# Layer 1's value windows, asked for by pairs of key chunks

## The chip, the cores and the metric

The kernel runs on one core of a Trainium2 chip, in one launch, in float32. The metric is the device time of that launch in microseconds (us). Five engines work side by side: TensorE (PE in the profile, with its weight loads as PEld), VectorE (DVE), ScalarE (ACT), GpSimd (POOL) and SyncE (SP). SP issues all of this kernel's DMAs.

## The reference

Sixteen images of 64 x 64 positions with 256 channels go through two layers. Each adds an attention to its input, and each normalises the input first in groups of 8 channels.

```python
# layer 0: linear attention over all 4096 positions, 8 heads of 32
q, k, v = split(gn(x) @ w_qkv)
q = softmax(q, over the head's 32) * SCALE
k = softmax(k, over the positions)
x = x + (v^T k applied to q) @ w_out
# layer 1: every position attends to the 7 x 7 window around it, 8 heads of 32
q, k, v = gn(x) @ Wq + bq, gn(x) @ Wk + bk, gn(x) @ Wv + bv
scores = q . (unfold(k, 7) + positional embedding)
x = x + softmax(scores, over 49) applied to unfold(v, 7)
```

## The kernel before

**The image's way.** One image at a time is held in SBUF as two tiles of 128 channels x 4096 positions (`img`). Positions are ordered by columns of eight; a strip is 512 of them, 256 KB for one half of the channels. For an image the stages are: `layer0`, which takes sixteen pairs of 128 tokens (`queries_keys`, then `context`) and then adds its output; statistics and positional products; `values`, which computes layer 1's values and stores them in DRAM in `vpad`, padded; `keys_queries` and `local_attention` for the first four heads (hg 0); the same two for the last four (hg 1). The work of the next image that can be done early is put between the steps of `local_attention`.

**`local_attention`.** The image's width is cut in four units of 16 columns, taken in the order `UNITS`. A unit has nine key chunks c of eight rows, taken in five groups g of two (the last has one). The loop runs over the 20 pairs (i, g) of unit and group and four more steps. In step n TensorE computes the scores of group n (L834, `pd` from `qq` and `kaug`), ACT their exponentials; then TensorE the products with the values of group n-1 (L878, "held"), and the sums of group n-2 (L908, "late"); DVE adds overlapping rows of neighbouring chunks (L863). When a unit's last group is through, ACT copies the products out of PSUM (L970), and in the following steps `finish` transposes and inverts the sums on DVE (L915 to L921), multiplies and adds on POOL (L934, L942) and calls `stored`, which issues the output's DMAs.

**The value windows.** A unit's values are one tile `vw` of 128 partitions x 2304 numbers, laid out `p (j c d)`: two blocks j of columns, nine chunks c, 128 channels d. `load_window` (L795) fills one by four DMAs of 288 KB in rows of 512 bytes. There are two buffers (pool `vwin`). The windows of units 0 and 1 of hg 0 are asked for ahead of `keys_queries`; window i+2 when unit i has been read; those of hg 1's units 0 and 1 in `between0`, two steps after hg 0's units 2 and 3 have been read. The same two buffers also hold the tokens of layer 0 (four blocks q of eight tiles, 1 MB, `load_tokens` at L457, with a column of ones that POOL sets at L460) and its output weights `w4`.

**What sets the order.** All engines but POOL follow the program's order (`manual_schedule`), and each engine's queue is in order. So on SP a DMA that waits, for a buffer that TensorE still reads or for an output that POOL has not finished, holds up all DMAs behind it. A DMA's completion is told by one of eight semaphores, taken in turn.

**Between the steps.** `between0(i, g)` is called each step of hg 0 with the "late" pair: it asks for half 1 of the next image strip by strip in units 0 and 1 (L1074), and takes its statistics in units 2 and 3. `between1` does it for hg 1: at (0, 0) it asks for the whole of half 0 (`load_half`, eight strips, L455), in unit 1 it takes the statistics, in units 2 and 3 the sums over groups and the first normalisation, and at the ends of units 2 and 3 it asks for token blocks 0 and 1 of the next image. `store_out` (L1060) issues a unit's one to three output strips together.

```python
                if held:
                    i, g, es = held
                    for c, e in es:
                        weighted(c, e, vw[i])
                    if g == 4:
                        ...
                        vw.pop(i)
                        if i + 2 < 4:
                            vw[i + 2] = load_window(b, hg, UNITS[i + 2])
```

Of the kernel before, what the change touches and what calls it, by code (L numbers as in the profile page):

```python
# [10 lines left out]
F32 = mybir.dt.float32  # L11
# [346 lines left out]
def attention_fast(tc, io, ok):  # L358
# [3 lines left out]
    with ExitStack() as ctx:  # L362
# [69 lines left out]
        tail = ctx.enter_context(tc.tile_pool(name="tail", bufs=1))  # L432
        vwin = ctx.enter_context(tc.tile_pool(name="vwin", bufs=2))
        small = ctx.enter_context(tc.tile_pool(name="small", bufs=2))

        def work_tile(name):
            return work.tile([P, 1024], F32, tag="work", name=name)

        def window(name):
            return vwin.tile([P, 2 * NB * P], F32, tag="vw", name=name)  # L440

# [10 lines left out]
        def load_half(b, k):  # L452
            x = halves(b)[0][k]
            for s in ORDER:
                nc.sync.dma_start(x[:, strip(s)], xc[b, :, k, strip(s)])  # L455

        def load_tokens(b, q):  # L457

            t = window(f"xtok{b}_{q}")[:, : 8 * (C + 1)].rearrange("p (t c) -> p t c", c=C + 1)
            nc.gpsimd.memset(t[:, :, C : C + 1], 1.0)  # L460
            nc.sync.dma_start(t[:, :, :C], xt[b, q])
            return t

# [50 lines left out]

        def layer0(b, x, xn, mean, rstd, xtok, ready, midway=None):

# [29 lines left out]
            def context(p):  # L546
                for t in range(2):
                    for hg in range(2):
                        nc.tensor.matmul(  # L549
                            pc[hg][:, : C + 1],  # L550
                            eq[p][:, t, C + hg * P : C + (hg + 1) * P],
                            xtok[p // 4][:, 2 * (p % 4) + t],
                            start=(p == 0 and t == 0),
                            stop=(p == 15 and t == 1),
                        )
# [8 lines left out]
            for p in range(16 + 1):  # L564
                if p < 16:
                    if p % 2 == 0 and p // 2 + 1 < NS and p // 2 + 1 >= ready:
                        normalise(xn, x, mean, rstd, ORDER[p // 2 + 1])
                    eq[p] = queries_keys(p)
                if p == 1:
                    mu = n.spread(mean, lambda name: other[1], small, f"{b}")  # L570
                if 1 <= p <= 16:
                    context(p - 1)
                    if p % 4 == 0 and p // 4 + 1 < 4:
                        xtok[p // 4 + 1] = load_tokens(b, p // 4 + 1)
                if p >= 2:
                    turned(p - 2)
                if p == 9 and midway:
                    fill()
# [42 lines left out]
            for hg in range(2):  # L621
                nc.vector.tensor_copy(z[:, hg], pc[hg][:, C : C + 1])
            w4 = window(f"w4_{b}")[:, : 8 * C].rearrange("p (h g c) -> p h g c", h=4, g=2)
            for h in range(2):
# [169 lines left out]

        def load_window(b, hg, t):  # L795


            vw = window(f"vw{b}_{hg}_{t}").rearrange("p (j c d) -> p j c d", j=2, d=P)
            v = vpad[b % 2]
            for j in range(2):  # L800
                for e, u in enumerate((2 * t + 2 * j, 2 * t + 1)):
                    row = v[u, 0, 0, hg * P : (hg + 1) * P]
                    src = bass.AP(row.tensor, row.offset, [[C, 64], [64 * C, NB], [1, P]])
                    nc.sync.dma_start(vw[64 * e : 64 * e + 64, j], src)
            return vw

        def local_attention(b, hg, x, y, vw, queries, after_scores, between, stored):

# [70 lines left out]

            def weighted(c, e, vw):  # L880
                if c == 0:

                    for i, to in enumerate(outs):
                        rows = slice(64 * i, 64 * i + 64)
                        nc.tensor.matmul(to, nb[rows], bits[rows, :1].to_broadcast([64, 512]), start=True, stop=False)
                for j in range(2):
                    for h in range(4):
                        v = vw[:, j, c, h * HD : (h + 1) * HD]
                        products(outs[j], j, h, c, e, *span(c), v, start=False, stop=(c == NB - 1))
# [64 lines left out]
            for step in range(len(groups) + 4):  # L954
                new = None
                if step < len(groups):
                    i, g = groups[step]
                    new = (i, g, [(c, scores(UNITS[i], c)) for c in range(2 * g, min(2 * g + 2, NB))])
                    if step == 0:
                        next(queries, None)  # L960
                    if step == len(groups) - 1:
                        after_scores()
                if held:
                    i, g, es = held
                    for c, e in es:
                        weighted(c, e, vw[i])
                    if g == 4:
                        rs[i] = [tail.tile([P, 2, 512], F32, tag=f"tail{k}", name=f"r{b}_{hg}_{i}_{k}") for k in range(2)]
                        for j in range(2):
                            nc.scalar.copy(rs[i][1][:, j], outs[j])  # L970
                        vw.pop(i)
                        if i + 2 < 4:
                            vw[i + 2] = load_window(b, hg, UNITS[i + 2])
                if late:
                    i, g, es = late
                    for c, e in es:
                        summed(c, e)
# [12 lines left out]
                held, late = new, held  # L990
# [3 lines left out]
        with tc.manual_schedule(engines=ORDERED):  # L994
# [6 lines left out]
            gn = n.group_stats(st, 1e-5, small, bank, "0_0")  # L1001
            xtok = {q: load_tokens(0, q) for q in range(2)}
            for s in ORDER[:2]:
# [14 lines left out]
            for b in range(B):  # L1018
                more = b + 1 < B
                x, xn = halves(b)  # L1020
                st = layer0(b, x, xn, *gn, xtok, 2, None if b else midway)
                load_weights(wk, "wk")
# [27 lines left out]
                fold_bias(mean, wq, (2, 3), pb)  # L1050
                vw = {i: load_window(b, 0, UNITS[i]) for i in range(2)}
                if more:
# [4 lines left out]
                y = [xn[0], x[1]]  # L1057
                vw1 = {}

                def store_out(hg, i):  # L1060

                    for s in ((3,), (4, 5), (6, 7), (1, 2, 0))[i]:
                        nc.sync.dma_start(out[b, :, hg, strip(s)], y[hg][:, strip(s)])

                def between0(i, g):
                    if more and i == 0 and g == 0:
                        load_weights(wv, "wv")
                    if g == 4:
                        if i >= 2:
                            vw1[i - 2] = load_window(b, 1, UNITS[i - 2])  # L1070
                    if more and g < 4:
# [5 lines left out]

                local_attention(b, 0, x, y, vw, queries, lambda: load_rings(1), between0, lambda i: store_out(0, i))
                queries = keys_queries(b, 1, x)
                next(queries)  # L1080
                steps, gn, xtok = None, [], {}

                def between1(i, g):
                    nonlocal steps
                    if g == 4:
                        if more and i >= 2:
                            xtok[i - 2] = load_tokens(b + 1, i - 2)
                    if not more:
                        return
                    if i == 0 and g == 0:  # L1090
                        load_weights(wq, "wq")
                        load_half(b + 1, 0)
                    if i == 1 and g < 4:
                        for s in ORDER[2 * g : 2 * g + 2]:
                            strip_stats(st, x_next, 0, s)
# [6 lines left out]

                local_attention(b, 1, x, y, vw1, queries, lambda: None, between1, lambda i: store_out(1, i))

# [386 lines left out]
```

## Time and profile before

| what | value |
|---|---|
| time, median of 3 runs | 5863.13 us (5862.11 to 5906.18) |
| the profiled execution's own span | 5890.5 us; no other time of that execution is given |
| busy PE, PEld | 5235.4 us (89%), 3609.8 us (61%) |
| busy DVE, ACT, POOL | 3439.0 us (58%), 2193.7 us (37%), 1335.2 us (23%) |
| DMA traffic | 540.80 MB, mean 92 GB/s |
| DMA issues: `vw`, tokens, strips of an image, outputs | 512 of 288 KB, 64 of 1024 KB, 256 of 256 KB, 256 of 256 KB |

The profile is of one execution. A line of a group or of a wait names engine, line of the kernel and tiles (out<-in), and then gives total us, number, and the longest or the mean. "issue" as the reason of a wait means that no semaphore of the program explains it. In the DMA views q1 is the queue of the kernel's own DMAs and q8 that of instructions; shares are of 16 DMA engines, and can pass 100% in a short stretch, since a packet counts where it begins.

### The profile page before, as it was taken

The page shows a single profiled execution, that of the slowest core. Times are in us where ns is not written, and L with a number is a line of the kernel's source. Part 1 is how long each engine was busy: PE and PEld are TensorE (multiplying, and loading weights), DVE is VectorE, ACT ScalarE, POOL GpSimd, SP SyncE. Part 2 cuts the span into 40 slices and gives each one's busy share as a digit, 9 for nine tenths or more (in the row PEclk, how much of TensorE's full clock was granted, in tenths as well). Part 3 has the DMA queues.
Part 4 walks back from the last instruction along what each step waited for, and adds up shares of the span by engine and source line. Part 5 has one row for each costly group of instructions (what it writes and reads, how often), then busy time and mean ns, then how long its engine had stood idle before and what let it go on. Part 6 is the DMA issues. An engine that isn't in the chain of part 4 may idle for free.

```text
span 5890.5 us, 169110 instructions
## 1 busy us (share of the span) xinstructions
PE 5235.4 (89%) x75313; PEld 3609.8 (61%) x75313; DVE 3439.0 (58%) x5946; ACT 2193.7 (37%) x3089; POOL 1335.2 (23%) x1946
## 2 busy tenths in 40 slices
PE   7889898898998989989889998988989989899997
PEld 4656566566665666656656666565665666656665
DVE  4565655656565565655655556565574655656555
ACT  1341624425144251442514325144351433514335
POOL 3031231302212022130221302213032130321303
PEclk9999999999999999999999999999999999999999
DMA  4543616445173451734517345173451734517344
GB/s 121 107 102 56 133 54 116 101 74 119 42 130 96 76 115 35 131 94 77 117 33 131 94 77 117 33 133 92 79 119 32 136 86 81 114 35 135 87 77 86
DMA packets 751604, 540.80 MB, mean 92 GB/s; under 512 B 241408, under 2 KB 682368, under 8 KB 748416
## 3 DMA queue, kind: packets, MB, share of 16 engines
q1 hardware_dynamic: 750864, 529.89, 44.1%
q8 instruction: 592, 9.70, 0.7%
q14 instruction: 148, 1.21, 0.1%
HBM read 371.04 MB, written 158.73 MB: 90 GB/s over the span
## 4 chain that ended last, share of the span: by engine, by line
PE 77%; DVE 8%; ACT 5%; issue 5%; DMA 2%; SPq 1%; POOL 1%; DVEq 0%; ACTq 0%; POOLq 0%
PE pd L531 15%; PE pd L834 13%; PE ps L878 8%; PE pd L771 7%; PE ps L549 6%; PE ps L771 5%; ACT qq L684 4%; PE ps L642 4%; PE pd L743 4%; PE pd L642 4%; PE ps L743 4%; PE ps L908 4%; DVE e L863 3%; PE ps L695 2%; DMA vpad<-v 1%
## 5 line engine op out<-in xcount | busy, mean ns | idle before, releaser
L863 DVE TENSOR_TENSOR e<-e,e 128x384 f32<-128x384 f32 x1024 | 732.4, 742 | 773.1 <-PE ps L878 615.2
L834 PE MATMUL pd<-qq,kaug 64*64 64x112 f32 (+4 forms) x27648 | 938.0, 277 | 159.8 <-issue 71.1
L834 PEld LDWEIGHTS pd<-qq,kaug 64*64 64x64 f32 x27648 | 813.2, 139 | 319.5 <-issue 181.8
L531 PE MATMUL pd<-wqkv,img 128*128 128x512 f32 x2048 | 948.8, 608 | 3.2 <-DVE img L285 3.2
L443 POOL TENSOR_TENSOR others<-others,rc 128x32 f32<-128x32 f32 x128 | 32.1, 251 | 2858.6 <-DVE rc L919 2858.4
L535 ACT ACTIVATE eq<-pd 128x1024 f32<-128x1024 f32 x256 | 261.9, 1023 | 1077.7 <-PE pd L531 1077.7
L531 PEld LDWEIGHTS pd<-wqkv,img 128*128 128x128 f32 x2048 | 399.1, 196 | 412.1 <-issue 376.6
L878 PE MATMUL ps<-e,vw 128*32 128x112 f32 (+1 forms) x18432 | 575.2, 261 | 65.2 <-issue 64.5
L538 DVE TENSOR_REDUCE qz<-eq 128x16 f32<-128x512 f32 x256 | 175.5, 686 | 766.9 <-ACT eq L535 766.9
L846 ACT ACTIVATE e<-pd 128x896 f32<-128x896 f32 (+2 forms) x576 | 461.4, 836 | 430.5 <-PE pd L834 423.5
L843 ACT ACTIVATE e<-pd 128x896 f32<-128x896 f32 (+2 forms) x576 | 462.4, 838 | 400.7 <-PE pd L834 395.8
L684 ACT ACTIVATE qq<-ps,bias 32x512 f32<-32x512 f32 (+2 forms) x512 | 318.6, 648 | 733.5 <-PE ps L695 668.6
L908 PE MATMUL ps<-e,ones 128*32 128x128 f32 (+2 forms) x10240 | 404.2, 266 | 146.3 <-DVE e L863 113.0
L878 PEld LDWEIGHTS ps<-e,vw 128*32 128x32 f32 x18432 | 419.0, 114 | 154.4 <-issue 117.5
L942 POOL TENSOR_TENSOR img<-img,r 128x320 f32<-128x320 f32 (+1 forms) x512 | 493.2, 993 | 0.0
L549 PE MATMUL ps<-xtok,eq 128*128 128x257 f32 x2048 | 483.4, 380 | 0.0
L549 PEld LDWEIGHTS ps<-xtok,eq 128*128 128x128 f32 x2048 | 387.4, 190 | 149.8 <-issue 107.1
L684 ACT ACTIVATE kaug<-pd,bias 32x512 f32<-32x512 f32 x256 | 173.7, 678 | 674.8 <-PE pd L771 671.9
L686 DVE TENSOR_SCALAR qq<-ps,bias 32x512 f32<-32x512 f32 (+2 forms) x416 | 312.3, 759 | 151.0 <-PE ps L771 145.2
L934 POOL TENSOR_TENSOR r<-r,r 128x512 f32<-128x512 f32 x256 | 340.7, 1352 | 140.5 <-DVE r L921 134.8
L908 PEld LDWEIGHTS ps<-e,ones 128*32 128x32 f32 x10240 | 253.3, 116 | 189.6 <-DVE e L863 148.1
L465 DVE BATCH_NORM_STATS2 st<-img 128x6 f32<-128x512 f32 x512 | 332.1, 679 | 9.7 <-DMA img<-in_xc 5.2
(128 smaller groups left out, 6609.9 us busy)
## 6 DMA issues: line engine op xcount, KB each, us to landing
vw<-vpad SPq DMA_DIRECT2D x512, 288.0 KB
img<-in_xc SPq DMA_DIRECT2D x256, 256.0 KB
xtok<-in_xt SPq DMA_DIRECT2D x64, 1024.0 KB
out<-img SPq DMA_DIRECT2D x256, 256.0 KB
vpad<-v SPq DMA_DIRECT2D x112, 512.0 KB
qq<-pos SPq DMA_DIRECT2D x128, 256.0 KB
qq<-in_ring SPq DMA_DIRECT2D x128, 256.0 KB
pos<-qq SPq DMA_DIRECT2D x128, 112.0 KB
```

Of the source, the lines that this page charges most:

```text
L531: nc.tensor.matmul(ps[:, t], xn[k][:, n0 : n0 + P], n.wqkv_sb[:, k, : 2 * C], start=(k == 0), stop=(k == 1))
L549: nc.tensor.matmul(pc[hg][:, : C + 1], eq[p][:, t, C + hg * P : C + (hg + 1) * P], xtok[p // 4][:, 2 * (p % 4) + t], start=(p == 0 and t = ...
L642: nc.tensor.matmul(py[a], w4[rows, h, hg, co * P : (co + 1) * P], qv[rows, 4 * hg + h, 8 * HD * i : 8 * HD * (i + 1)], start=(h == 0 and h ...
L684: nc.scalar.activation(dst, src, AF.Identity, bias=bias)
L743: nc.tensor.matmul(pi[:, t], x[k][:, n0 : n0 + P], wv[:, k], start=(k == 0), stop=(k == 1))
L771: nc.tensor.matmul(ps[a], wgt[:, k, hg * P : (hg + 1) * P], x[k][:, strip(pair[a])], start=(k == 0), stop=(k == 1),)
L834: nc.tensor.matmul(to, kaug[pl][rows, u, 8 * c : 8 * c + 8].rearrange("p r w -> p (r w)"), q, start=True, stop=True,)
L843: nc.scalar.activation(e.rearrange("p (a n) -> p a n", a=2), ps[:, :, : 2 * m], AF.Exp)
L863: nc.vector.tensor_tensor(part, part, rows_of(c - 1, before, r0, 8 * c), ALU.add)
L878: nc.tensor.matmul(dst, stationary, pr, **flags)
L908: nc.tensor.matmul(dst, ones, pr, start=True, stop=True)
L942: nc.gpsimd.tensor_tensor(yv, xv, by_rows(add[:, :, a - w0 : e - w0], xv), ALU.add)
```

## The change

The two window buffers become plain tiles `vbuf[0]` and `vbuf[1]`, laid out `p (c j d)`, so that a pair of chunks is one piece. `load_window(b, k, g)` fills group g of window k (k = 0 to 7 over both halves of the heads) by four DMAs of 64 KB (32 KB for the last group). In each step, after the products of group (i, g), a function `read(i, g)` asks for the same group of the window two units on: hg 1's first two windows follow hg 0's last two. In the second half's units 2 and 3, where no window is left, it asks for the tokens of the next image, one or two tiles at a time; in layer 0 token blocks 2 and 3 are asked for two tiles at a time, each after the tiles in its place have been read. The strips of half 0 come one a step in place of all at once, and their statistics a step later. Outputs that are ready are put in a list `leaving`, from which `send` issues one a step, at the start of `between0` and `between1`.

```diff
+        vbuf = [cp.tile([P, 2 * NB * P], F32, tag=f"vbuf{i}", name=f"vbuf{i}") for i in range(2)]
...
+        windows = [v.rearrange("p (c j d) -> p c j d", j=2, d=P) for v in vbuf]
+
+        def tokens_of(q):
+            return vbuf[q % 2][:, : 8 * (C + 1)].rearrange("p (t c) -> p t c", c=C + 1)
+
+        def load_tokens(b, q, t0=0, t1=8):
+            t = tokens_of(q)
+            nc.gpsimd.memset(t[:, t0:t1, C : C + 1], 1.0)
+            nc.sync.dma_start(t[:, t0:t1, :C], xt[b, q, :, t0:t1])
...
                     context(p - 1)
-                    if p % 4 == 0 and p // 4 + 1 < 4:
-                        xtok[p // 4 + 1] = load_tokens(b, p // 4 + 1)
+                    q = (p - 1) // 4 + 2
+                    if q < 4:
+                        load_tokens(b, q, 2 * ((p - 1) % 4), 2 * ((p - 1) % 4) + 2)
...
-        def load_window(b, hg, t):
-            vw = window(f"vw{b}_{hg}_{t}").rearrange("p (j c d) -> p j c d", j=2, d=P)
+        def load_window(b, k, g):
+            t = UNITS[k % 4]
             v = vpad[b % 2]
+            c0, m = 2 * g, min(2, NB - 2 * g)
+            vw = windows[k % 2]
             for j in range(2):
                 for e, u in enumerate((2 * t + 2 * j, 2 * t + 1)):
-                    row = v[u, 0, 0, hg * P : (hg + 1) * P]
-                    src = bass.AP(row.tensor, row.offset, [[C, 64], [64 * C, NB], [1, P]])
-                    nc.sync.dma_start(vw[64 * e : 64 * e + 64, j], src)
+                    row = v[u, 8 * c0, 0, (k // 4) * P : (k // 4 + 1) * P]
+                    src = bass.AP(row.tensor, row.offset, [[C, 64], [64 * C, m], [1, P]])
+                    nc.sync.dma_start(vw[64 * e : 64 * e + 64, c0 : c0 + m, j], src)
...
-                        v = vw[:, j, c, h * HD : (h + 1) * HD]
+                        v = windows[i % 2][:, c, j, h * HD : (h + 1) * HD]
...
                     for c, e in es:
-                        weighted(c, e, vw[i])
+                        weighted(i, c, e)
+                    read(i, g)
...
-                        vw.pop(i)
-                        if i + 2 < 4:
-                            vw[i + 2] = load_window(b, hg, UNITS[i + 2])
...
-                vw = {i: load_window(b, 0, UNITS[i]) for i in range(2)}
+                for k in range(2):
+                    for g in range(5):
+                        load_window(b, k, g)
...
                 def store_out(hg, i):
-                    for s in ((3,), (4, 5), (6, 7), (1, 2, 0))[i]:
+                    leaving.extend((hg, s) for s in ((3,), (4, 5), (6, 7), (1, 2, 0))[i])
+
+                def send():
+                    if leaving:
+                        hg, s = leaving.pop(0)
                         nc.sync.dma_start(out[b, :, hg, strip(s)], y[hg][:, strip(s)])
 
+                def read0(i, g):
+                    load_window(b, i + 2, g)
+
                 def between0(i, g):
+                    send()
...
-                    if g == 4:
-                        if i >= 2:
-                            vw1[i - 2] = load_window(b, 1, UNITS[i - 2])
...
+                def read1(i, g):
+                    if i < 2:
+                        load_window(b, i + 6, g)
+                    elif more:
+                        t0, t1 = ((0, 1), (1, 3), (3, 5), (5, 7), (7, 8))[g]
+                        load_tokens(b + 1, i - 2, t0, t1)
 
                 def between1(i, g):
                     nonlocal steps
-                    if g == 4:
-                        if more and i >= 2:
-                            xtok[i - 2] = load_tokens(b + 1, i - 2)
+                    send()
                     if not more:
                         return
                     if i == 0 and g == 0:
                         load_weights(wq, "wq")
-                        load_half(b + 1, 0)
-                    if i == 1 and g < 4:
-                        for s in ORDER[2 * g : 2 * g + 2]:
+                    n0 = 5 * i + g
+                    if n0 < NS:
+                        nc.sync.dma_start(x_next[0][:, strip(ORDER[n0])], xc[b + 1, :, 0, strip(ORDER[n0])])
+                    if i == 1 and g > 0:
+                        for s in ORDER[2 * g - 2 : 2 * g]:
                             strip_stats(st, x_next, 0, s)
```

What is still in `leaving` is sent after hg 1's first `keys_queries` part and at the end of the image. The arithmetic of the kernel and the order of PE's, DVE's and ACT's instructions stay, but for the statistics of half 0.

More of the change, by code (lines that the diff above doesn't have):

```diff
@@ L432, in attention_fast @@
         tail = ctx.enter_context(tc.tile_pool(name="tail", bufs=1))
-        vwin = ctx.enter_context(tc.tile_pool(name="vwin", bufs=2))
+        vbuf = [cp.tile([P, 2 * NB * P], F32, tag=f"vbuf{i}", name=f"vbuf{i}") for i in range(2)]
         small = ctx.enter_context(tc.tile_pool(name="small", bufs=2))
@@ L437, in work_tile @@
             return work.tile([P, 1024], F32, tag="work", name=name)
-        def window(name):
-            return vwin.tile([P, 2 * NB * P], F32, tag="vw", name=name)
         def watch(total, x, w):
@@ L450, in halves @@
             return [img[0][0], img[1][b % 2]], [img[0][1], img[1][1 - b % 2]]
[L452 to L462, printed above, removed]
+        windows = [v.rearrange("p (c j d) -> p c j d", j=2, d=P) for v in vbuf]
[5 more added lines that the diff above has]
+            nc.sync.dma_start(t[:, t0:t1, :C], xt[b, q, :, t0:t1])
         def strip_stats(st, x, k, s):
@@ L513, in fill, with layer0 @@
                         nc.sync.dma_start(dst, zero[:, : (w1 - w0) * C])
-        def layer0(b, x, xn, mean, rstd, xtok, ready, midway=None):
+        def layer0(b, x, xn, mean, rstd, ready, midway=None):
             mu = None
@@ L551, in context @@
                             eq[p][:, t, C + hg * P : C + (hg + 1) * P],
-                            xtok[p // 4][:, 2 * (p % 4) + t],
+                            tokens_of(p // 4)[:, 2 * (p % 4) + t],
                             start=(p == 0 and t == 0),
@@ L622, in layer0 @@
                 nc.vector.tensor_copy(z[:, hg], pc[hg][:, C : C + 1])
-            w4 = window(f"w4_{b}")[:, : 8 * C].rearrange("p (h g c) -> p h g c", h=4, g=2)
+            w4 = vbuf[0][:, : 8 * C].rearrange("p (h g c) -> p h g c", h=4, g=2)
             for h in range(2):
@@ L793, in keys_queries, with local_attention @@
                                 evacuate(engines[a], dst, src, bias[rows, 2 * what + hg : 2 * what + hg + 1])
-        def load_window(b, hg, t):
-            vw = window(f"vw{b}_{hg}_{t}").rearrange("p (j c d) -> p j c d", j=2, d=P)
+        def load_window(b, k, g):
+            t = UNITS[k % 4]
             v = vpad[b % 2]
+            c0, m = 2 * g, min(2, NB - 2 * g)
+            vw = windows[k % 2]
             for j in range(2):
                 for e, u in enumerate((2 * t + 2 * j, 2 * t + 1)):
-                    row = v[u, 0, 0, hg * P : (hg + 1) * P]
-                    src = bass.AP(row.tensor, row.offset, [[C, 64], [64 * C, NB], [1, P]])
-                    nc.sync.dma_start(vw[64 * e : 64 * e + 64, j], src)
-            return vw
-        def local_attention(b, hg, x, y, vw, queries, after_scores, between, stored):
+                    row = v[u, 8 * c0, 0, (k // 4) * P : (k // 4 + 1) * P]
+                    src = bass.AP(row.tensor, row.offset, [[C, 64], [64 * C, m], [1, P]])
+                    nc.sync.dma_start(vw[64 * e : 64 * e + 64, c0 : c0 + m, j], src)
+        def local_attention(b, hg, x, y, queries, after_scores, read, between, stored):
             outs, zs = single[:2], single[2:]
@@ L878, in products, with weighted @@
                 nc.tensor.matmul(dst, stationary, pr, **flags)
-            def weighted(c, e, vw):
+            def weighted(i, c, e):
                 if c == 0:
-                    for i, to in enumerate(outs):
-                        rows = slice(64 * i, 64 * i + 64)
+                    for a, to in enumerate(outs):
+                        rows = slice(64 * a, 64 * a + 64)
                         nc.tensor.matmul(to, nb[rows], bits[rows, :1].to_broadcast([64, 512]), start=True, stop=False)
@@ L1001, in attention_fast @@
             gn = n.group_stats(st, 1e-5, small, bank, "0_0")
-            xtok = {q: load_tokens(0, q) for q in range(2)}
+            for q in range(2):
+                load_tokens(0, q)
             for s in ORDER[:2]:
@@ L1020, in attention_fast @@
                 x, xn = halves(b)
-                st = layer0(b, x, xn, *gn, xtok, 2, None if b else midway)
+                st = layer0(b, x, xn, *gn, 2, None if b else midway)
                 load_weights(wk, "wk")
@@ L1057, in attention_fast @@
                 y = [xn[0], x[1]]
-                vw1 = {}
+                leaving = []
                 def store_out(hg, i):
-                    for s in ((3,), (4, 5), (6, 7), (1, 2, 0))[i]:
+                    leaving.extend((hg, s) for s in ((3,), (4, 5), (6, 7), (1, 2, 0))[i])
+                def send():
+                    if leaving:
+                        hg, s = leaving.pop(0)
                         nc.sync.dma_start(out[b, :, hg, strip(s)], y[hg][:, strip(s)])
+                def read0(i, g):
+                    load_window(b, i + 2, g)
                 def between0(i, g):
+                    send()
                     if more and i == 0 and g == 0:
                         load_weights(wv, "wv")
-                    if g == 4:
-                        if i >= 2:
-                            vw1[i - 2] = load_window(b, 1, UNITS[i - 2])
                     if more and g < 4:
@@ L1076, in between0 @@
                             strip_stats(st, x_next, 1, s)
-                local_attention(b, 0, x, y, vw, queries, lambda: load_rings(1), between0, lambda i: store_out(0, i))
+                local_attention(b, 0, x, y, queries, lambda: load_rings(1), read0, between0, lambda i: store_out(0, i))
                 queries = keys_queries(b, 1, x)
                 next(queries)
-                steps, gn, xtok = None, [], {}
+                while leaving:
+                    send()
+                steps, gn = None, []
+                def read1(i, g):
[4 more added lines that the diff above has]
+                        load_tokens(b + 1, i - 2, t0, t1)
                 def between1(i, g):
                     nonlocal steps
-                    if g == 4:
-                        if more and i >= 2:
-                            xtok[i - 2] = load_tokens(b + 1, i - 2)
+                    send()
                     if not more:
@@ L1101, in between1 @@
                         normalise(xn_next, x_next, *gn, ORDER[g - 1])
-                local_attention(b, 1, x, y, vw1, queries, lambda: None, between1, lambda i: store_out(1, i))
+                local_attention(b, 1, x, y, queries, lambda: None, read1, between1, lambda i: store_out(1, i))
+                while leaving:
+                    send()
             m = small.tile([P, 4], F32, tag="range", name="range")
```

## The prediction

> **What bounds the kernel now.** I read the page first, then PE's waits, then one image on the timeline (2588 to 2955 us), then the DMA queues inside it.
>
> ```profile
> span 5890.5 us, 169110 instructions
> ...
> PE 5235.4 (89%) x75313; PEld 3609.8 (61%) x75313; DVE 3439.0 (58%) x5946; ACT 2193.7 (37%) x3089; POOL 1335.2 (23%) x1946
> ...
> q1 hardware_dynamic: 750864, 529.89, 44.1%
> q8 instruction: 592, 9.70, 0.7%
> ```
>
> TensorE is the bound at 89%, and the kernel's own transfers fill 44% of the DMA engines. The last line matters most: 592 packets and 9.70 MB, 16 KB each, are instructions being fetched. TensorE has 2 x 75313 matmuls and weight loads[...].
>
> An image takes 354 to 374 us (the first 390). Of that the two runs of `local_attention`, from their first score product on, take 69.0 us (first half of the heads, to the next `keys_queries`) and 74.1 us (second half, to the next image's first product) on the mean of images 2 to 15. A step of the loop is about 2.7 us. In PE's waits these lines belong to those two stages:
>
> ```profile
> PE pd L834 <- issue: 71.1, 53, 3.0
> ...
> PE ps L878 <- issue: 64.5, 50, 3.6
> ...
> PE ps L908 <- issue: 31.5, 21, 3.7
> ```
>
> "issue" is a wait that no semaphore explains. Together they are 167.1 us in 124 stalls of up to 3.7 us: the largest idle time in the loop. One of them on the timeline of PE, with SP's queue before it:
>
> ```profile
> 2800.17 3.22 SPq L804 DMA_DIRECT2D vw<-vpad  x4
> ...
> 2807.37 0.78 PE L878 MATMUL ps<-e,vw 128*32 128x112 f32 x24
> 2810.67 0.46 PE L878 MATMUL ps<-e,vw 128*32 128x112 f32 x8 [2.52 <-issue]
> ```
>
> TensorE stops after 24 of 32 equal matmuls, operands all present, for 2.52 us. The DMA queues in 2802.5 to 2807.8 and in 2807.8 to 2809.4:
>
> ```profile
> q1 hardware_dynamic: 2099, 1.14, 120.0%
> ...
> q1 hardware_dynamic: 219, 0.37, 80.3%
> q8 instruction: 1, 0.02, 5.0%
> ```
>
> While the four window DMAs (4 x 288 KB) drained at 215 GB/s no instruction packet ran; the next one started at 2808.03, 6.8 us after the one before it, where a quiet stretch has one every 3.5 us; TensorE went on 2.6 us after its start. So the stall is TensorE waiting for instructions behind a block of value tiles.
>
> I then counted all 382 fetches inside the two stages in the trace's packet records. The time at which a fetch is due follows from how many instructions TensorE has issued. Sorted by what q1 carried at that time:
> - nothing (196 fetches): 0.22 us late in the median, 0.13 us of stall on the mean;
> - 512-byte packets, the value windows (111): 1.62 us late, 1.23 us of stall, 137 us in all;
> - 2 KB packets, strips and stores (48): 0.51 us late, 0.38 us, 18 us;
> - 1 KB packets, tokens (27): 1.09 us late, 0.30 us, 8 us.
>
> Their lateness fits the share of one DMA on one engine: a window DMA has 576 packets, 36 on each of 16 engines, at 48 ns (two or more in flight) 1.7 us; a strip has 8 of 88 ns, 0.7 us. Tokens would have 64 of 48 ns, 3 us, and reach 3.35 us in the worst tenth.
>
> [...]the clock record has 0.5 for 3.41 us right after the stall above; mean clock in the two stages is 0.95 and 0.92.
>
> **The change part by part.**
>
> *Windows by pairs of chunks.* Each window of 4 DMAs of 288 KB becomes five groups of 4, 64 KB each (32 KB for the last), 512 to 2560 DMAs. Bytes and 512-byte packets are the same. A DMA leaves 8 packets on an engine instead of 36: 8 x 48 ns = 0.4 us, so a fetch that meets one should be late as one that meets a strip. A piece is 256 KB, 1.0 to 1.3 us at 200 to 250 GB/s, in each 2.7 us step, so more fetches meet some: I take 150 (bounds 111 and 230) with 0.35 us each (from the strips' 0.38). That is 53 us for 137: 84 us less. Stage time against issue stalls over images 2 to 15 has slope 1.39 in the first half and 0.86 in the second, the half clock being part of it; at 1.2 this is 101 us.
>
> *Tokens in pieces.* Two tiles per DMA instead of eight: 16 packets on an engine, 0.8 us. 27 fetches go from 0.30 to about 0.2 us: 3 us. In layer 0 pieces are asked for 8 pairs ahead of their use (5 to 8 before), and a pair takes 5.2 us: no wait. The eight strips of the next image, formerly at once at the start of the second half, go one a step: same packets, 0 us.
>
> *First windows.* 40 DMAs instead of 8 before `keys_queries`, ordered so that what is read first lands first. SP needs 40 x 0.4 = 16 us where it needed 7.3; the first group is read 20 us after the start, the next ones 2.7 us apart. `PE pd L951 <- DMA vw<-vpad: 11.8` should go: 12 us.
>
> *New waits on TensorE.* Two matmuls of each group wait for two DMAs, instead of two of each window: 1280 double waits for 256, 1024 more semaphore instructions. One takes 51 ns, two in a row are 139 ns apart. In the first chunk such a wait stands at the 17th of 32 weight loads, and the run is not longer for it (36 ns steps on both sides)[...]. Bounds 0 and 142 us (1024 x 139 ns); I take 10. What is behind such a wait is all of TensorE, but its data was asked for ten steps (27 us) before.
>
> *SP's queue.* A step now issues 4 window pieces, up to one strip and one store: 6 x 0.34 to 0.45 us = 2.4 us of 2.7. It is moved past the stores' wait for POOL:
>
> ```profile
> SPq L1063 <- POOL img L942: 1226.6, 176, 14.5
> ```
>
> About 6 us each time a unit of columns is finished; behind it now stand two steps of windows and strips, which come out as a block of 1 to 1.3 MB, but of small DMAs. Windows have 27 us to spare. The tightest is strip 7 in the second half: asked for at step 9 behind the blocked store, read by DVE's statistics at step 11. I get it landing 1 to 1.5 us after DVE wants it; behind DVE stands L863, whose result TensorE needs one step later, so nearly all is hidden: 5 us over 15 images, bounds 0 and 40.
>
> *POOL.* In the second half a memset of 0.12 us per piece waits for TensorE ahead of a unit's finishing work, which can start about 1 us later; its result is stored, and ACT's copy at L970 waits for it after the last scores. The next layer 0 runs 9 us of L531 before it needs those banks. 0 us; if that cover went, 1 us an image.
>
> Sum: 101 + 3 + 12 - 10 - 5 = 101 us, span 5790. The page gives this execution's span and no other time of it; the runs' median is 0.9954 of the span. 5863 x 5790/5890.5 = 5763 us.
>
> **Rivals.**
>
> *A. The stalls go altogether.* With 0.4 us per DMA the fetch may come in time, as in the quiet case. Then 111 x (1.23 - 0.13) + 10 = 132 us at 1.39, plus 12, less 15: 180, giving 5684. For it: quiet fetches have a slack that takes 0.22 us. Against: strips, 0.7 us per DMA, still cost 0.38.
>
> *B. Most of the gain is lost again in SP's blocks.* If two steps' pieces released together hold a fetch up as a window did, a third of the gain is left: 34 + 12 - 20 = 26 us, giving 5837. For it: 176 such waits of 7 us. Against: lateness of strips did not grow when eight lay queued at once (about 1 us at 2894).
>
> *C. Slower: the delay is per meeting, not per size.* If any 512-byte traffic, whatever its DMA's size, makes a fetch 1.6 us late[...], spreading only makes more fetches meet it: about 0.6 x 382 = 230 x 1.23 = 283 us for 137, with 3 us of new waits net: +149 us, giving 6011. It decides from 137/230 = 0.6 us of stall per meeting on.[...] Against: the strips' 0.51 us at equal bytes.
>
> **How the numbers follow.** Forecast 0.50 (5715 to 5810), A 0.14, B 0.20, C 0.16. The range 5670 to 5880 holds the first three and leaves C out. A change of under 1% (below 59 us) can't be told from none here. Faster by more: A, nearly all of the forecast and a little of B, 0.63; within 1%: most of B, 0.20; slower: C and the worst of the semaphores, 0.17.
>
> **What would show it.** Right: "issue" of PE at the scores, products and sums falls from 167 us to about 70; the two stages shorten to about 65 and 71 us; clock in them rises; PE's wait for the windows at L951 is gone; layer 0, values and `keys_queries` keep their times. The 2.6 us from a fetch's start to PE's going on stays. Wrong: as many or more stalls, now of 0.5 to 1.5 us in most steps (C); blocks of stalls three steps after each unit's end (B); PE waiting for DMA at the products, or DVE for a strip (SP too slow); weighted runs of 32 matmuls longer than 0.72 us (semaphores).

## The result: slower, 6089 us

The changed kernel takes 6089.05 us (median of 4 runs, 6076.65 to 6094.63); the kernel before, beside it, 5884.66 us (5862.11 to 5916.67). The ratio is 1.0334, interval 1.0282 to 1.0386: slower by about 200 us, where 100 us less was predicted.

First the page of the changed kernel: span, busy engines, the queues of the kernel's data (q1) and of instructions (q8), and the chain that ended last, by engine.

```profile
span 6085.1 us, 173815 instructions
...
PE 5279.8 (87%) x75313; PEld 3619.4 (59%) x75313; DVE 3493.3 (57%) x5946; ACT 2198.4 (36%) x3089; POOL 1378.7 (23%) x2162
...
q1 hardware_dynamic: 787088, 530.04, 38.5%
q8 instruction: 596, 9.76, 0.7%
...
PE 67%; DVE 10%; DMA 7%; SPq 6%; issue 4%; ACT 4%; POOL 2%; DVEq 0%; ACTq 0%; POOLq 0%
```

The same last line of the kernel before:

```profile
PE 77%; DVE 8%; ACT 5%; issue 5%; DMA 2%; SPq 1%; POOL 1%; DVEq 0%; ACTq 0%; POOLq 0%
```

TensorE's share of the chain falls by ten points, and DMA and SP's queue, 3% together before, carry 13%. The bytes are the same (530 MB). So the kernel waits for transfers now, not because more is moved. PE's and DVE's waits of the changed kernel (us, times, longest us) say which:

```profile
DVE st L461 <- DMA img<-in_xc: 122.2, 51, 4.3
PE pd L831 <- DMA qq<-in_ring: 117.6, 34, 4.6
...
PE pd L831 <- issue: 23.2, 47, 1.5
...
PE ps L875 <- issue: 18.8, 32, 2.1
...
PE ps L905 <- issue: 12.8, 26, 1.6
```

The last three answer to the 167.1 us shown of before: 54.8 us, less even than the 70 predicted. The first two are new: 117.6 us in which the scores wait for the ring rows of `qq`, none before, and 122.2 us in which DVE's statistics wait for a strip of the next image (about 5 before). The ring rows hold the positional part of the queries and constants; `load_rings` fills them for the second half by eight DMAs, which can be asked for only after the first half's last scores, and the second half's first scores read them. By stages (mean of images 2 to 15; a stage is read as in the prediction, `keys_queries` is that between the halves):

| | before | predicted | after |
|---|---|---|---|
| first half of the heads | 69.0 us | 65 us | 65.7 us |
| `keys_queries` between | 27.4 us | the same | 27.7 us |
| second half | 74.1 us | 71 us | 90.3 us |
| clock, first and second half | 0.946, 0.921 | higher | 0.980, 0.833 |

The first half does what was predicted. The loss is in the second: 16.2 us an image, 3.3 of it paid back by the first and 0.3 added in `keys_queries`. Over 16 images that would make 16 x 13.2 = 211 us, against 195 us between the two spans.

Why ring rows and strips come late is on SP's queue at the turn from the first half to the second. Start, duration, line, tiles and number of equal instructions, changed kernel:

```profile
2918.76 3.47 SPq L802 DMA_DIRECT2D vbuf<-vpad  x4
2922.28 0.59 SPq L1077 DMA_DIRECT2D img<-in_xc  x1
2922.97 3.46 SPq L802 DMA_DIRECT2D vbuf<-vpad  x4
2926.53 0.54 SPq L1065 DMA_DIRECT2D out<-img  x1
2927.11 1.37 SPq L1077 DMA_DIRECT2D img<-in_xc  x1
...
2949.75 11.38 SPq L802 DMA_DIRECT2D vbuf<-vpad  x16
2961.22 0.54 SPq L1065 DMA_DIRECT2D out<-img  x1
2961.86 0.38 SPq L728 DMA_DIRECT2D qq<-pos  x1
...
2968.88 4.57 SPq L729 DMA_DIRECT2D qq<-in_ring  x1
```

and before:

```profile
2849.72 1.27 SPq L731 DMA_DIRECT2D qq<-pos  x1
```

The two steps shown first take SP 4.2 us (four pieces and a strip) and 5.6 us (with a store). On the mean of the first half's steps SP takes 3.7 us and TensorE 3.0, breaks at the ends of units counted in. The half's last sums are over at about 2948, and SP still has 16 pieces to issue, with no wait over 0.4 us between them, before it comes to the rings. In the kernel before it starts them 68.7 us after the half's first score product (2781), here 79.5 us after (2882.4).

How far SP is behind can be read group by group, from the end of TensorE's products to the start of the first piece that takes their place (mean of images 2 to 15). At the first group of the half it is 6 us, since the 40 pieces of the first two windows, ahead of the half, took SP 27 us; by the eighteenth group the steps have made it 18 us. SP catches up in the `keys_queries` between the halves, and in the second half it falls 12 us behind again. TensorE, where the rings are late:

```profile
2975.15 0.43 PE L831 MATMUL pd<-qq,kaug 64*64 64x64 f32 x12
2979.32 0.44 PE L831 MATMUL pd<-qq,kaug 64*64 64x64 f32 x2 [3.74 <-DMA qq<-in_ring]
2983.77 1.99 PE L831 MATMUL pd<-qq,kaug 64*64 64x64 f32 x34 [4.00 <-DMA qq<-in_ring]
```

7.7 us are lost in two waits. The lateness goes on: 40 us later DVE stands for a strip, and behind it L860, for which TensorE's sums wait (195.8 us in all, 113.0 before):

```profile
3025.27 0.69 DVE L461 BATCH_NORM_STATS2 st<-img 128x6 f32<-128x512 f32 x1 [4.35 <-DMA img<-in_xc]
```

The price behind it stands in the list of each line's instructions (nanoseconds least, median, most), in the changed kernel

```profile
L802 SPq DMA_DIRECT2D vbuf<-vpad x2560: 444/600/2318, 224.8 to 6046.2; - x197
```

and, readable beforehand, in the kernel before:

```profile
L804 SPq DMA_DIRECT2D vw<-vpad x512: 573/638/4508, 225.8 to 5846.9; - x171
```

To issue a window DMA cost SP 0.638 us in the median for 288 KB and 0.600 us for the pieces, most of 64 KB. An image has 160 now and had 32: 96 us of SP for 20. Strips went from 0.43 to 0.59 us, stores from 0.34 to 0.49. In the kernel before, a store and a strip read

```profile
L1063 SPq DMA_DIRECT2D out<-img x256: 332/344/5226, 276.2 to 5884.6; - x128
L1074 SPq DMA_DIRECT2D img<-in_xc x120: 327/432/2428, 235.7 to 5395.8; - x120
```

And SP no longer waits much at the stores: its wait for POOL ahead of a store, 1226.6 us before, is now

```profile
SPq L1065 <- POOL img L939: 136.3, 23, 12.5
```

With stores sent in the same way, but whole windows (e4_whole below), it is 773.1 us. So SP comes to most stores when POOL has long been done.

### The profile page after: what moved, and what is told of

It is laid out like the page before. It is cut to its first block, busy times and chain, and to the rows that moved or that the text cites. A ratio compares the mean times of both kernels' runs of the same rounds, so it can differ in the third digit from the quotient of the medians.

```text
span 6085.1 us, 173815 instructions
## 1 busy us (share of the span) xinstructions
PE 5279.8 (87%) x75313; PEld 3619.4 (59%) x75313; DVE 3493.3 (57%) x5946; ACT 2198.4 (36%) x3089; POOL 1378.7 (23%) x2162
## 4 chain that ended last, share of the span: by engine, by line
PE 67%; DVE 10%; DMA 7%; SPq 6%; issue 4%; ACT 4%; POOL 2%; DVEq 0%; ACTq 0%; POOLq 0%
PE pd L527 15%; PE pd L831 11%; PE ps L545 6%; PE ps L875 6%; PE pd L768 5%; PE ps L768 4%; DMA qq<-in_ring 4%; PE ps L639 4%; PE pd L639 4%; PE pd L740 3%; DVE e L860 3%; PE ps L740 3%; PE ps L905 3%; SPq L802 3%; ACT qq L681 2%
## 5 line engine op out<-in xcount | busy, mean ns | idle before, releaser
L831 PE MATMUL pd<-qq,kaug 64*64 64x112 f32 (+4 forms) x27648 | 953.4, 278 | 227.0 <-DMA qq<-in_ring 117.6
L860 DVE TENSOR_TENSOR e<-e,e 128x384 f32<-128x384 f32 x1024 | 777.8, 789 | 648.5 <-PE ps L875 494.2
L905 PE MATMUL ps<-e,ones 128*32 128x128 f32 (+2 forms) x10240 | 407.6, 266 | 222.3 <-DVE e L860 195.8
L875 PE MATMUL ps<-e,vbuf 128*32 128x112 f32 (+1 forms) x18432 | 564.7, 259 | 20.1 <-issue 18.8
L939 POOL TENSOR_TENSOR img<-img,r 128x320 f32<-128x320 f32 (+1 forms) x512 | 508.6, 1023 | 0.0
L875 PEld LDWEIGHTS ps<-e,vbuf 128*32 128x32 f32 x18432 | 412.7, 112 | 123.1 <-issue 74.0
L545 PE MATMUL ps<-vbuf,eq 128*128 128x257 f32 x2048 | 483.6, 380 | 0.0
L545 PEld LDWEIGHTS ps<-vbuf,eq 128*128 128x128 f32 x2048 | 387.6, 190 | 149.8 <-issue 107.2
L461 DVE BATCH_NORM_STATS2 st<-img 128x6 f32<-128x512 f32 x512 | 335.9, 682 | 126.8 <-DMA img<-in_xc 122.2
L931 POOL TENSOR_TENSOR r<-r,r 128x512 f32<-128x512 f32 x256 | 357.1, 1415 | 140.2 <-DVE r L918 132.6
```

Of the source, the lines that this page charges most:

```text
L545: nc.tensor.matmul(pc[hg][:, : C + 1], eq[p][:, t, C + hg * P : C + (hg + 1) * P], tokens_of(p // 4)[:, 2 * (p % 4) + t], start=(p == 0 an ...
L831: nc.tensor.matmul(to, kaug[pl][rows, u, 8 * c : 8 * c + 8].rearrange("p r w -> p (r w)"), q, start=True, stop=True,)
L860: nc.vector.tensor_tensor(part, part, rows_of(c - 1, before, r0, 8 * c), ALU.add)
L875: nc.tensor.matmul(dst, stationary, pr, **flags)
L905: nc.tensor.matmul(dst, ones, pr, start=True, stop=True)
L939: nc.gpsimd.tensor_tensor(yv, xv, by_rows(add[:, :, a - w0 : e - w0], xv), ALU.add)
```

## Experiments

Three theories went into the runs. The first: SP's queue is too slow because of the number of window DMAs, and rings and strips are issued late. The second: SP is held by its waits, at the stores for POOL and at the pieces for TensorE, with everything behind them. The third: the pacing of strips, tokens and stores does it, not the windows. Each kernel ran beside the kernel before (5882.3 us for e1 to e6, 5882.0 us for f7 to f10). Stages are those of the table above; fetch lateness is the median beside 512-byte packets, counted as in the prediction (the moment at which a fetch is due is the author's estimate from TensorE's instruction count: 150626 matmuls and weight loads to 592 instruction packets in the kernel before, 254 to a packet; so read it as small or large, not to the hundredth); "issue" is PE's at scores, products and sums.

| kernel | window DMAs | ratio to before (95%) | first / second half, us | "issue", us | PE on rings, us | fetch lateness, us |
|---|---|---|---|---|---|---|
| before | 512 | 1 | 69.0 / 74.1 | 167 | 0 | 1.62 |
| after | 2560 | 1.0334 (1.0282 to 1.0386) | 65.7 / 90.3 | 55 | 117.6 | 0.39 |
| e1_halves | 1024 | 0.9976 (0.9954 to 0.9998) | 69.3 / 72.1 | 111 | 0 | 0.61 |
| e4_whole | 512 | 1.0017 (1.0004 to 1.0031) | 70.2 / 73.5 | 182 | 0 | 1.97 |
| e6_single | 4608 | 1.2327 (1.2282 to 1.2371) | 97.9 / 113.4 | 26 | 494.1 | 0.59 |
| e2_rings | 2560 | 1.0717 (1.0678 to 1.0756) | 66.1 / 80.7 | 50 | 0 | 0.35 |
| f10_poolstore | 2560 | 1.0268 (1.0237 to 1.0298) | 65.7 / 88.1 | 55 | 76.7 | 0.45 |
| f8_split | 1024 | 0.9906 (0.9875 to 0.9937) | 65.5 / 72.3 | 67 | 0 | 0.63 |

**e1_halves: fewer, larger pieces.** After, with a window in two groups of four DMAs, asked for at its second and its fifth step:

```diff
+            if g not in (1, 4):
+                return
-            c0, m = 2 * g, min(2, NB - 2 * g)
+            c0, m = (0, 4) if g == 1 else (4, 5)
```

> The changed kernel with windows in two pieces of four and five chunks (8 DMAs of 128 and 160 KB a window, 1024 in all) in place of five of two chunks (20 of 64 KB, 2560). Theory 1, SP's issue time: a window DMA costs SP 0.60 us whatever its size (0.60 after, 0.64 before), 96 us an image after; that makes SP late and with it the ring loads and strips. Then 38 us an image is few enough: TensorE's wait for ring loads (about 112 us) goes to under 15, DVE's wait for strips (122 us) to under 30, and instruction stalls at scores, products and sums come out between before (167 us) and after (55 us), about 90, lateness of a fetch beside 512-byte packets 0.8 to 1.0 us; 5760 to 5820 us. Rival 2, SP waits rather than works (each step's piece waits for TensorE, each store for POOL): waits are still there every two or three steps and at every store, so ring loads stay late; over 5980 us. Rival 3, pacing of strips, tokens and stores is what costs: no change, over 6050 us.

Measured: 5865.92 us. The ring wait is gone, DVE's wait for strips is back at 5.0 us, the second half at 72.1 us. With 1536 DMAs fewer on SP all of the loss is gone, as the first theory says. The gain was missed, and so was "issue" (111 us for about 90), which fell by 56 us from before where the time fell by 16. Where the rest went is taken up below.

**e4_whole: the pacing alone.** After, with each window asked for whole, by four DMAs at its fifth step:

```diff
+            if g < 4:
+                return
-                    row = v[u, 8 * c0, 0, (k // 4) * P : (k // 4 + 1) * P]
-                    src = bass.AP(row.tensor, row.offset, [[C, 64], [64 * C, m], [1, P]])
-                    nc.sync.dma_start(vw[64 * e : 64 * e + 64, c0 : c0 + m, j], src)
+                    row = v[u, 0, 0, (k // 4) * P : (k // 4 + 1) * P]
+                    src = bass.AP(row.tensor, row.offset, [[C, 64], [64 * C, NB], [1, P]])
+                    nc.sync.dma_start(vw[64 * e : 64 * e + 64, :, j], src)
```

> The changed kernel with whole windows (4 DMAs of 288 KB, 512 in all, in the new layout, asked for when a unit has been read); strips, tokens and stores one piece a step as after. Theory 1: SP has time again, ring and strip waits fall to what before has (0 and about 5 us), instruction stalls return to 140 to 170 us, fetch lateness beside 512-byte packets to about 1.6 us; 5850 to 5920 us. Rival 3, pacing of strips, tokens and stores is what costs: stays over 6000 us. Rival 2, waits on SP: the stores' and strips' waits are still there, 5950 to 6050 us.

Measured: 5893.59 us, ratio 1.0017. Strips, tokens and stores one a step, with the memsets, plain buffers and the new order, cost at most 0.3%. The third theory falls: the loss is in the windows' pieces. Stalls of 182 us are more than the 140 to 170 expected.

**e6_single: the dose raised.** After, with every chunk a group of four DMAs of its own:

```diff
+            for c in range(2 * g, min(2 * g + 2, NB)):
+                load_chunk(b, k, c)
+        def load_chunk(b, k, c0):
+            m = 1
-            c0, m = 2 * g, min(2, NB - 2 * g)
```

> The changed kernel with windows chunk by chunk: 36 DMAs of 32 KB a window, 4608 in all, still asked for once a step, so SP waits as often as after but issues 1.8 times as many. Theory 1: windows alone cost SP 173 us an image, more than the 185 us or so of the stages in which they are asked for leave beside rings, strips and stores; ring loads and strips come later still, 6500 to 7200 us. Rival 2, SP's waits and not its work: as after, 6050 to 6150 us. Instruction stalls stay at about 55 us or fall.

Measured: 7252.55 us. Its waits, and the issue price of its windows:

```profile
PE pd L834 <- DMA qq<-in_ring: 494.1, 64, 18.6
...
PE ps L878 <- DMA vbuf<-vpad: 377.5, 451, 3.5
```

```profile
L805 SPq DMA_DIRECT2D vbuf<-vpad x4608: 444/594/2210, 221.7 to 7215.1; - x192
```

A piece of 32 KB costs SP 594 ns, again the same. There are 2048 more than in the changed kernel: 2048 x 0.594 = 1217 us of SP, and the time grew by 1163 us. In the first half 144 pieces of 0.594 us make 86 of its 97.9 us: SP's issuing sets the pace there, and TensorE waits for the windows themselves too. By the second theory nothing should have changed; SP's waits for TensorE at the pieces did not grow (314.5 us, 341.1 in the changed kernel), its issuing did. "issue" is down to 26 us: the stalls the change set out to remove are nearly gone in the slowest kernel of all.

**e2_rings: the rings past SP's queue.** After, with the second half's ring loads issued by ACT:

```diff
+            issue = nc.scalar if hg else nc.sync
-                nc.sync.dma_start(...)
+                issue.dma_start(...)
```

> The changed kernel with the ring loads of the second half of the heads (8 DMAs an image) issued from ACT's queue and not SP's; all else as after. Theory 1: the ring loads no longer stand behind SP's windows, TensorE's wait for them (about 112 us, 7 us an image) goes to under 15; strips and their statistics stay late (122 us), so the time is 5950 to 6040 us, with ACT held some us an image by issuing. If the ring loads are late because the DMA engines are full and not because SP issues them late, the wait stays near 112 us and the time above 6070 us.

Measured: 6307.62 us, a miss. PE's ring wait is gone and the second half is 80.7 us, but `keys_queries` went from 27.7 to 51.5 us. PE's wait there, and an instance of what ACT did, on its timeline:

```profile
PE ps L769 <- ACT r L969: 315.1, 16, 23.5
```

```profile
3061.17 0.32 ACTq L729 DMA_DIRECT2D qq<-pos  x1
3068.00 0.33 ACTq L730 DMA_DIRECT2D qq<-in_ring  x1
...
3079.08 0.33 ACTq L730 DMA_DIRECT2D qq<-in_ring  x1
3079.51 1.07 ACT L969 COPY r<-ps 128x512 f32<-128x512 f32 x2 [36.39 <-DMA vbuf<-vpad]
```

Issuing a ring load costs ACT 0.33 us only, but the eight are spread over 18 us, and the trace names window DMAs as what released ACT. SP was still issuing the half's late windows then (to about 3071). So the ring loads were not freed of the lateness; ACT, idle 36.4 us before its copy, stood in it instead, with `keys_queries` behind it. That PE's wait on rings moved with the engine that issues them is in favour of the first theory; the time of this run cannot measure it. What ties ACT's issues to the windows was not tried.

**f10_poolstore: no store on SP.** After, with the outputs sent by POOL:

```diff
-                        nc.sync.dma_start(out[b, :, hg, strip(s)], y[hg][:, strip(s)])
+                        nc.gpsimd.dma_start(out[b, :, hg, strip(s)], y[hg][:, strip(s)])
```

> The changed kernel with the output stores issued from POOL's queue, where they stand behind the work that makes them; SP issues 16 DMAs less an image (8 us) and never waits for POOL's results at stores. Theory 1 (SP's issuing, 96 us an image for windows): ring loads and strips come only some 8 us earlier; TensorE's wait for rings falls from 112 to 20 to 70 us, DVE's wait for strips stays over 60 us; 5980 to 6060 us. Rival 2 (stores that wait in SP's order): both waits vanish, 5750 to 5850 us.[...]

Measured: 6046.84 us. SP issues no store and waits at none, and these waits stay:

```profile
DVE st L461 <- DMA img<-in_xc: 121.0, 53, 3.9
...
PE pd L831 <- DMA qq<-in_ring: 76.7, 24, 4.5
```

The strips are as late as before it, the rings a third less. 40 of some 200 us come back, less than the 125 us of SP that 16 stores an image of 0.49 us make. The second theory falls as far as the stores go; its other half, the waits at the pieces, was met by e6_single.

**f8_split: smaller DMAs at the old moment.** The kernel before, with each of its window DMAs cut in two and nothing else changed:

```diff
-                    src = bass.AP(row.tensor, row.offset, [[C, 64], [64 * C, NB], [1, P]])
-                    nc.sync.dma_start(vw[64 * e : 64 * e + 64, j], src)
+                    for c0, m in ((0, 4), (4, 5)):
+                        src = bass.AP(row.tensor, row.offset + 64 * C * c0, [[C, 64], [64 * C, m], [1, P]])
+                        nc.sync.dma_start(vw[64 * e : 64 * e + 64, j, c0 : c0 + m], src)
```

> The kernel before with each window DMA split by chunks in two (four and five chunks, 128 and 160 KB), all eight asked for one after the other at the old moment; nothing is spread over the steps. Size theory (a fetch of instructions waits for one DMA's share on its engine): 16 to 20 packets in place of 36, so lateness beside 512-byte packets falls from 1.62 us to 0.6 to 0.9 us in the median, and instruction stalls at scores, products and sums from 167 us to 100 to 120. Spreading theory (it is the pieces' distance in time that helped): lateness stays at 1.4 to 1.8 us and stalls over 150 us. Time 5830 to 5880 us by the first, as before by the second.

Measured: 5827.04 us, 0.9906, the fastest of those that leave no work out. PE's "issue":

```profile
PE ps L879 <- issue: 27.5, 40, 2.6
...
PE pd L835 <- issue: 20.0, 37, 1.5
...
PE ps L909 <- issue: 19.2, 25, 1.8
```

67 us for 167, less than the 100 to 120 expected. The windows still come as a block after each unit; only the size of one DMA is new: 16 or 20 packets on an engine for 36 (256 or 320 over 16 engines, for 576), and a fetch beside them 0.63 us late for 1.62. So here smaller DMAs made the fetches less late without being spread, and spreading is not needed for the gain. The 512-byte packets were also shorter, 27 ns in the median for 45, so there are two reasons for the shorter share. Of the 100 us of stalls that are gone, 55 show in the time.

**f7_nomul and f9_before_nomul: where e1's gain went.** ACT's copy of a unit's outputs waits for POOL's finish of the unit before. In e1_halves these waits came to 170 us (114.6 before), most of them this one:

```profile
ACT r L970 <- POOL img L941: 93.3, 49, 5.9
```

Both kernels, e1_halves (f7) and before (f9), lose the same instruction from POOL's finish:

```diff
-                    nc.gpsimd.tensor_tensor(pv, pv, rz, ALU.mult)
```

> The two-piece kernel (e1_halves) with POOL's multiplication by the inverse sums (L933, 2 x 1.4 us a unit) left out, so that a unit's finish is shorter by that and the output lacks the normalisation. e1 had 56 us less of instruction stalls than before and was only about 16 us faster; ACT's waits for POOL ahead of its copy of a unit's products rose from 115 to 170 us, and TensorE then waits for that copy (21 us, none before). If POOL's finish, which holds the one copy buffer, took the gain, then this is 40 us or more faster than e1 (5780 to 5830 us) and gains more than the same cut gains in the kernel before (f9). If not, both cuts gain the same, or nothing.

> The kernel before with the same multiplication on POOL left out (output without the normalisation): the control for f7. If POOL's finish binds only where the stalls have gone, 0 to 20 us faster than before; if it binds in both, about as much as f7 against e1.

Measured: 5673.71 us (0.9638, 0.9596 to 0.9679) and 5754.08 us (0.9780, 0.9742 to 0.9819). ACT's wait for POOL is about 1 us and 0. Leaving the multiplication out is worth 5866 - 5674 = 192 us in e1_halves, more than expected, and 5882 - 5754 = 128 us in before, where 0 to 20 or as much as in e1_halves was expected. So it costs time in both, which the prediction had not seen, and 64 us more once the fetch stalls are fewer: between f9 and f7 the halves bring 80 us, between before and e1_halves 16.

By which road it costs is not shown, since the cut does two things. It ends ACT's waits, and it also makes DVE's addition (L862), which TensorE's sums wait for, faster. In e1_halves and then in f7:

```profile
L862 DVE TENSOR_TENSOR e<-e,e 128x384 f32<-128x384 f32 x1024 | 767.0, 778 | 704.6 <-PE ps L877 534.0
L862 DVE TENSOR_TENSOR e<-e,e 128x384 f32<-128x384 f32 x1024 | 575.1, 590 | 796.1 <-PE ps L877 615.3
```

One addition took 0.56 us where POOL did nothing, and 1.24 us in the mean of the 198 that ran mostly beside POOL's multiplication (e1_halves). The sums waited 121.6 us for it in e1_halves and 34.0 us in f7; TensorE's own wait for ACT's copy was 21.4 us. And f8_split, 39 us faster than e1_halves, has as long a wait of ACT for POOL (180.9 us). So the copy buffer is not shown to have taken e1's gain. TensorE's gaps in the first half (mean of images 2 to 15, e1_halves against before) add up as follows: "issue" 1.6 us less, waits for DVE's addition 0.8 more, for ACT's copy 0.6 more, matmuls busy 0.3 longer, and the half is no shorter. A second copy buffer, which would take ACT's wait away without leaving work out, was not tried.

## Why the prediction was wrong

- *Smaller DMAs, fewer fetch stalls: right.* Lateness 0.39 us for the 0.4 predicted, "issue" 54.8 us for about 70, first half 65.7 us for 65. The 0.4 was luck in part: 8 packets of 48 ns were assumed, and a 512-byte packet took 27 ns in the median in the changed kernel (45 before), 0.2 us for eight. More fetches met window packets than assumed (251 for 150), each with 0.20 us of stall for 0.35. f8_split shows the smaller DMAs as the cause: 0.63 us late for 1.62, "issue" 67 us for 167. That a fetch waits for one DMA's share of an engine was the author's estimate, from 36 packets of 48 ns beside 1.62 us of lateness. Over the runs (packets of a window DMA over 16 engines) 36 give 1.62 and 1.97 us, 16 to 20 give 0.61 and 0.63, 8 give 0.35 to 0.45. With 4 (e6_single) it is 0.59, not less; how window packets hold a fetch up is not shown.
- *SP's queue: the step that failed.* "6 x 0.34 to 0.45 us = 2.4 us of 2.7", and for the first windows "40 x 0.4 = 16 us", gave the window pieces the price of stores (0.344 us) and strips (0.432 us). The row of the same instruction, 0.638 us for 288 KB, was in the profile and was not used; the price hardly shrinks with the bytes, 0.600 us for 64 KB. With strips and stores dearer as well a full step is 4 x 0.60 + 0.59 + 0.49 = 3.5 us, over the 2.7 of TensorE, and the 40 first pieces took 27 us. So SP falls behind in each half, and the rings are issued 11 us later than before. The term put at 5 us (bounds 0 and 40) became the whole loss: about 16 us an image in the second half.
- *"The tightest is strip 7": the wrong wait.* The strips were looked at for a block of two steps, and the rings, issued after all but the last two groups of pieces of the first half and read soonest after that, not at all. 117.6 us of PE's time went there, and DVE's 122.2 us at the strips was not hidden as supposed: sums waiting for L860 rose by 83 us. TensorE's gaps in the second half, after against before (mean of images 2 to 15), account for the 16.2 us within 0.4: 7.6 at the rings, 4.1 more at DVE's addition, 2.5 more at the sums over groups behind the strips' statistics (L268), 1.4 more at other waits for DVE and ACT, 2.9 less at "issue", and the same matmuls busy 3.8 us longer (64.2 for 60.4) at the lower clock (0.833 for 0.921).
- *First windows, tokens, semaphores, POOL.* The wait at `keys_queries` for the windows fell from 11.8 to 2.4 us, as said. e4_whole puts tokens, strips, stores and memsets together at +0.2%: nothing, as said. The first half came at the predicted length with all its double waits, which speaks for the 10 us taken and against 142; they were not measured by themselves.
- *Rivals.* A's mechanism half came (0.20 us of stall a meeting), C's did not come: 0.20 us is far from the 0.6 where it decides. B named SP's blocks, but as a cause of late fetches; they were one of late data. The slower side was given to C, at 6011 us: the sign had a chance of 0.17 for a reason that was false, and the true reason had a term with an upper bound of 40 us, some six times too small (16 x 16.2 = 259 us in the second half).
- *What would show it.* "PE waiting for DMA at the products, or DVE for a strip (SP too slow)" is what came, with the scores in place of the products.

Still open: why a window DMA costs SP 0.6 us where a token piece (256 KB) costs 0.378, and a ring load (`in_ring`) 2.9 us on SP but 0.34 on ACT (medians, after and e2_rings), and why strips and stores became dearer behind window pieces. The bytes of a window DMA are excluded by 32 to 288 KB; the shape of the access, or a full queue, was not tried apart. After the rings SP also stands at window pieces until ring loads have landed (84.7 us over the run); what that is worth was not separated. Open too is why e1_halves keeps more stalls than f8_split at the same DMA size (111 for 67 us): the two differ in layout, in spreading and in the pacing of strips, tokens and stores.

## What to carry to other kernels

Here cutting the window DMAs in two took PE's "issue" from 167 to 67 us, but each piece cost SP's queue about what a whole DMA had cost (0.594 to 0.638 us for 32 to 288 KB). So price a piece from the row of the same instruction, multiply by the pieces of a step, and hold the sum against the step. Then look for what is issued last behind them and read first, since that is what became late here (the rings, by 11 us). Cut as little as removes the stall: in f8_split two pieces took away 100 us of stalls where five took 112, with a quarter of the added DMAs.

## What was not expected of the hardware

- To issue a window DMA took SP 0.638, 0.616, 0.600 and 0.594 us for 288, 128 to 160, 64 and 32 KB. For 64 KB that is longer than the time that the packets take on an engine (an estimate, 0.2 us: 128 packets over 16 engines, 8 of 27 ns each; the way to landing is not in it), and over the whole range the price falls by 0.044 us.
- In the second half, with 68 waits of over 2 us in 14 images (up to 5.6 us), TensorE had a mean clock of 0.833, against 0.980 in the first half of the same images, which had one such wait.
- POOL, busy 23% of the span, had one multiplication whose absence was worth 128 us of 5882. DVE's addition took 0.56 us beside an idle POOL, 1.19 us in the mean beside that multiplication and 1.01 us beside POOL's addition (kernel before); a single buffer between ACT's copy and POOL's finish is the other road, and the two were not separated.
